# Three banks for the block sums, two for the direct sums, and POOL copying the codes of its rows

## The chip, the cores and the metric

The kernel runs on one core of a Trainium2 chip. The metric is the device time of one execution in microseconds (us), as the median of ten runs. Five engines run side by side, each through its own list of instructions in order: PE (TensorE, matrix products), DVE (VectorE), ACT (ScalarE), POOL (GpSimd) and SP (SyncE, which here only issues transfers). Transfers run on 16 DMA engines that all queues share.

## The reference

A graph layer with 6,250 nodes of 128 features and 206,250 edges. Each edge has a row of 128 numbers, which is added to the row of its source node; the node rows then go through a small network and a layer norm:

```
edge_aggr = jnp.zeros((n, HIDDEN), dtype=x.dtype).at[row].add(edge_features)
combined = jnp.concatenate([x, edge_aggr, global_expand], axis=-1) @ W_c + b_c
h = jax.nn.softplus(combined @ W1 + b1)
h = jax.nn.softplus(h @ W2 + b2)
return h @ W3 + b3
...
x = _layernorm(x + _L0_gnn_ref(x, edge_index, edge_attr_128, ...), axis=-1)
```

Nearly all the time goes into the first line, the sum of 206,250 rows by source node.

## The kernel before

**The sum by node.** The 6,250 nodes are cut into 25 blocks of `BL` = 256 nodes. The sum of each block stands transposed in SBUF, as 256 columns of `sums_t` (128 features on the partitions). An edge row is added to its block with a product on PE: the weights are 128 edge rows (edges on the partitions, features along), the moving side is a 0/1 matrix `hot` of 128 edges by 256 nodes with a one where the edge's node is. That needs 128 edges of one block together, and the edges come in no order. So the edges go through DRAM:

- The edges lie as 1,612 columns of 128. The first 48 columns (`DIRECT`) are treated apart. The other 1,564 are cut into ten groups g0 to g9 of 40, 120, 200, 240, 240, 240, 212, 140, 88 and 44 columns (`GROUPS`).
- `positions(g)` counts on PE and DVE where each edge of a group goes, so that the edges of one block lie together. It ends in a table `pos`. Its count matrices use two PSUM tiles called `pr` (two banks) and two called `small`.
- A group is loaded in pieces of ten columns (`LOAD_COLS`), 159 in all: `load_rows` (issued by SP, `LEAD` = 3 pieces ahead, five buffers) brings 10 x 128 edge rows of 128 numbers into `rows`. `code_rows` copies one number for each edge, the code `low` that says which node of the block it is, into the 129th column of `rows` (line 599, on ACT, two pieces ahead). `scatter_rows` issues, on POOL, one indirect transfer for each column (line 607): 128 rows of 129 numbers go to the places that `pos` names in a DRAM buffer `place`. There are three such buffers, filled ahead with -1 (`fill_rows`).
- `reduce_steps(g)` reads a scattered group back by loads of 1,024 rows (`load`, two ahead, four buffers `chunks`). `match` compares on DVE the 129th number of every row with 256 node numbers and gives `hot` (line 406, two buffers). `total` multiplies on PE (line 421), two block sums to a PSUM tile `part` (two buffers), and adds each to `sums_t` on DVE (line 426). `sub`, the chunk in columns, is 1, 2 or 4 by group: a load holds 8, 4 or 2 sums.

**The direct columns.** `direct_steps` makes for the first 48 columns a `direct_hot` of 128 x 512 on ACT (lines 540 and 542, three buffers), for all 13 windows of nodes, multiplies on PE (line 552) into one PSUM bank `direct_sum`, and adds that on DVE (line 556).

**The node rows.** `node_rows` prepares during one group (g3) what the network needs of `x` (28 steps with 13 loads of `x`, transposes and products in `small` tiles).

**The order of the work.** PE, DVE, ACT and SP run in the order in which the program writes the instructions down. The loop at line 659 goes through the groups, and in each through its pieces: after `load_rows(i + 3)`, `code_rows(i + 2)` and `scatter_rows(i)` of a piece it writes a share of four lists of steps: `prep` (the positions of g+1), `sums` (`reduce_steps(g - 1)`), `other` (the node rows) and `filled` (the filling). `AHEAD` says at which share of the group's pieces each list is to be through. A share of the direct steps, by the weights `left`, comes with them. Behind the loop the sums of g9 follow (line 689), and then the network and the layer norm (lines 693 to 823).

Of the kernel before, what the change touches and what calls it, by code (L numbers as in the profile page):

```python
# [7 lines left out]
F32 = mybir.dt.float32  # L8
# [28 lines left out]
AHEAD = (0.75, 0.95, 0.9, 0.75)  # L37
# [8 lines left out]
def kernel(  # L46
# [119 lines left out]
    with ExitStack() as phase:  # L166
# [4 lines left out]
        chunks_p = phase.enter_context(tc.tile_pool(name="chunks", bufs=4))  # L171
        direct_p = phase.enter_context(tc.tile_pool(name="direct", bufs=1))
        hots = phase.enter_context(tc.tile_pool(name="hots", bufs=2))
# [7 lines left out]
        low = keep.tile([P, TC], F32, name="low")  # L181
# [54 lines left out]
        def positions(g):  # L236
# [86 lines left out]
            def place(k, j0, j1):  # L323
                m = j1 - j0
                pr = by_col(ps.tile([P, 512], F32, name="pr", bufs=2))[:, :, :m]
                nc.tensor.matmul(pr, upto_h, in_block[k][1][:, :, j0:j1], start=True, stop=False)  # L326
                nc.tensor.matmul(pr, ones_h, so_far[k][:, :, j0:j1], start=False, stop=False)  # L327
                nc.tensor.matmul(
                    pr, ones_h, got["more", k].unsqueeze(2).to_broadcast([P, NB, m]),
                    start=False, stop=False)  # L330
                nc.tensor.matmul(pr, scale_h,  # L331
                                 got["begin"].unsqueeze(2).to_broadcast([2, NB, m]),
                                 start=False, stop=True)
                got[k, j0] = pr
# [49 lines left out]
        def reduce_steps(g):  # L384
# [26 lines left out]
            def total(i):  # L411
                s0, k = loads[i]
                _, at = nc.values_load_multi_w_load_instructions(
                    offs_of[g][:, s0:s0 + k], engines=[DVE], min_val=0, max_val=(NB - 1) * BL,
                    skip_runtime_bounds_check_because="it is held under the last block")
                t, hot = chunks.pop(i), hot_of.pop(i)
                for q in range(0, k, 2):
                    part = ps.tile([P, 2, BL], F32, name="part", bufs=2)
                    for s in range(q, min(k, q + 2)):
                        for j in range(sub):  # L420
                            nc.tensor.matmul(part[:, s - q, :], t[:, s * sub + j, :D],  # L421
                                             hot[:, s * sub + j],
                                             start=(j == 0), stop=(j == sub - 1))
                    for s in range(q, min(k, q + 2)):
                        here = sums_t[:, bass.ds(at[s], BL)]
                        nc.vector.tensor_add(here, here, part[:, s - q, :])  # L426
# [3 lines left out]
            for i in range(min(2, n)):  # L430
                steps.append(lambda i=i: load(i))
            for i in range(n + 1):
                def one(i=i):
                    if i + 2 < n:
                        load(i + 2)
                    if i < n:
                        match(i)
                    if i:
                        total(i - 1)
                steps.append(one)  # L440
            return steps
# [66 lines left out]
        def direct_steps():  # L508
# [26 lines left out]
            def compare(c, w, q):  # L535
                n = min(WIDE, NB * BL - w * WIDE)
                hot = direct_p.tile([P, QUAD, WIDE], F32, name="direct_hot", bufs=3)
                hot_of[c, w, q] = hot
                for j in range(QUAD):
                    nc.scalar.activation(hot[:, j, :n], iota_f[:, :n], AF.Abs,  # L540
                                         bias=less[:, w, c + q + j:c + q + j + 1], scale=-1.0)
                nc.scalar.activation(hot[:, :, :n], hot[:, :, :n], AF.Relu, bias=ones[:, :1],  # L542
                                     scale=-1.0)

            def add(c, w, q):
# [3 lines left out]
                if q == 0:  # L549
                    sum_of[c, w] = ps.tile([P, WIDE], F32, name="direct_sum", bufs=1)  # L550
# [44 lines left out]
        def code_rows(i):  # L595
            if i >= len(pieces):
                return
            g, c, k, r = pieces[i]
            nc.scalar.copy(rows_at[i][:r, :k, D:W], low[:r, c:c + k].unsqueeze(2))  # L599
# [15 lines left out]
        with tc.manual_schedule(engines={ET.PE, ET.DVE, ET.Activation, ET.SP}):  # L615
# [23 lines left out]
            for i in range(LEAD - 1):  # L639
                code_rows(i)  # L640
# [13 lines left out]
            for g in range(1, G - 3):  # L654
                left[g] = max(0.0, groups[g][1] - groups[g][0]
                              - groups[g - 1][3] * groups[g - 1][2] / 3 - (26 if g == 3 else 0))
            direct_at = 0.0
            i = 0
            for g in range(G):
# [5 lines left out]
                other = node_rows() if g == min(3, G - 1) else []  # L665
                filled = fill_rows(g + 1)
                done = [0, 0, 0, 0]
                for q in mine:
                    load_rows(i + LEAD)
                    code_rows(i + LEAD - 1)  # L670
# [4 lines left out]
                    for w, todo in enumerate((prep, sums, other, filled)):  # L675
                        share = min(1.0, (q - mine[0] + 1) / (AHEAD[w] * len(mine)))
                        upto = int(round(len(todo) * share))
                        now.append(todo[done[w]:upto])
                        done[w] = upto
# [168 lines left out]
```

## Time and profile before

| what | value |
|---|---|
| median of ten runs | 2167.57 us (2164.63 to 2169.86) |
| the profiled execution | 2164.48 us |
| its span in the trace | 2162.7 us |
| granted TensorE clock, mean | 0.915 |
| PE busy | 1768.3 us (82%) |
| PE weight loads busy | 1185.8 us (55%) |
| POOL busy | 1555.0 us (72%) |
| DVE busy | 1382.0 us (64%) |
| ACT busy | 814.6 us (38%) |
| first scatter of line 607 begins | 26.54 us |
| last scatter ends | 2007.56 us |

The profile lists, for each line of the kernel and each engine, the number of instructions, their busy time, the mean of one, and the idle time of the engine just before them with what ended it ("issue" is a wait that the profile has no releaser for). A timeline gives the same instructions in order. Busy time of POOL is what the profiler counts for an instruction; the time from one start to the next can be longer.

### The profile page before, as it was taken

The numbers are of one execution on the slowest core, as the hardware profiler recorded it, in microseconds if no ns is written. First come the engines' busy times: TensorE is split into PE (matmuls) and PEld (weight loads), VectorE is DVE, ScalarE is ACT, GpSimd is POOL, SyncE is SP. The second block draws the span as 40 slices with busy tenths as digits, with TensorE's granted clock in tenths as the row PEclk, the third lists the DMA queues.
The fourth block names the chain that finished last, engine by engine and source line by source line (L and its number), as shares of the span: only waits on it lengthen the run. The fifth ranks groups of instructions, "written<-read, shape, count | busy, mean of one in ns | idle before, by whom it ended". The sixth has DMA issues, their size and how long they took to land.

```text
span 2162.7 us, 22153 instructions
## 1 busy us (share of the span) xinstructions
PE 1768.3 (82%) x6415; PEld 1185.8 (55%) x6415; DVE 1382.0 (64%) x1943; ACT 814.6 (38%) x1174; POOL 1555.0 (72%) x1631
## 2 busy tenths in 40 slices
PE   3399798857999959999769998499993898688885
PEld 0144355534656636666446666276762777567643
DVE  7386376424767537776347764277662788798877
ACT  0367675652434444545443454434431000000034
POOL 5677777777777777777777777777777777777126
PEclk8699899978999979999979999799996999899997
DMA  9999788738888657566456555465654787787421
GB/s 290 301 302 289 204 260 255 241 100 250 252 232 254 177 151 216 190 201 215 130 181 200 191 180 174 136 211 191 198 193 141 218 232 225 197 217 203 119 81 60
DMA packets 415375, 435.49 MB, mean 201 GB/s; under 512 B 37743, under 2 KB 305766, under 8 KB 415254
## 3 DMA queue, kind: packets, MB, share of 16 engines
q1 hardware_dynamic: 365062, 330.71, 53.3%
q0 software_dynamic: 50048, 103.35, 14.4%
q8 instruction: 51, 0.84, 0.2%
q14 instruction: 70, 0.57, 0.1%
q10 hardware_dynamic: 144, 0.02, 0.0%
HBM read 260.90 MB, written 173.03 MB: 201 GB/s over the span
## 4 chain that ended last, share of the span: by engine, by line
PE 41%; DMA 19%; POOL 14%; DVE 11%; issue 10%; ACT 2%; SPq 2%; DVEq 0%; POOLq 0%; ACTq 0%
PE part L421 25%; POOL place L607 14%; PE direct_sum L552 13%; DMA place<-rows,pos 10%; DVE sums_t L426 4%; DMA chunks<-place 3%; DVE hot L406 3%; DMA x_sb<-in_x 2%; SPq L143 2%; DMA place<-fill 2%; DVE so_far L309 1%; DMA rows<-in_edge_attr 1%; PE pr L331 1%; ACT direct_hot L540 1%; ACT away L727 0%
## 5 line engine op out<-in xcount | busy, mean ns | idle before, releaser
L607 POOL DMA_INDIRECT place<-rows,pos x1564 | 1498.2, 958 | 502.2 <-issue 440.7
L421 PE MATMUL part<-hot,chunks 128*128 128x256 f32 x4472 | 1064.3, 393 | 199.5 <-DVE hot L406 167.5
L421 PEld LDWEIGHTS part<-hot,chunks 128*128 128x128 f32 x4472 | 864.5, 196 | 421.6 <-DVE hot L406 184.5
L406 DVE SCALAR_TENSOR_TENSOR hot<-chunks,iota_ps 128x2048 f32<-128x2048 f32 (+1 forms) x281 | 637.3, 2269 | 253.4 <-DMA chunks<-place 253.4
L540 ACT ACTIVATE direct_hot<-iota_f,less 128x512 f32<-128x512 f32 (+1 forms) x624 | 405.1, 696 | 679.2 <-PE direct_sum L552 676.4
L552 PE MATMUL direct_sum<-direct_hot,direct_rows 128*128 128x512 f32 (+1 forms) x1248 | 582.0, 599 | 65.1 <-DMA direct_rows<-in_edge_attr 26.6
L426 DVE TENSOR_TENSOR sums_t<-sums_t,part 128x256 f32 x781 | 327.8, 420 | 341.6 <-PE part L421 320.4
L552 PEld LDWEIGHTS direct_sum<-direct_hot,direct_rows 128*128 128x128 f32 x1248 | 239.1, 196 | 282.7 <-issue 227.2
L542 ACT ACTIVATE direct_hot<-direct_hot,ones 128x1024 f32<-128x1024 f32 (+1 forms) x312 | 348.1, 1116 | 10.1
L599 ACT COPY rows<-low 128x10 f32<-128x10 f32 (+1 forms) x159 | 31.1, 198 | 510.9 <-DMA place<-rows,pos 451.6
L342 DVE TENSOR_REDUCE pos<-at 128x20 int32<-128x500 f32 (+2 forms) x80 | 87.2, 1090 | 2.7
L309 DVE TENSOR_TENSOR_SCAN so_far<-iota_ps,ib 128x1500 bf16<-128x1500 f32 (+5 forms) x29 | 85.7, 2955 | 0.0
L556 DVE TENSOR_TENSOR sums_t<-sums_t,direct_sum 128x512 f32<-128x512 f32 (+1 forms) x52 | 34.6, 666 | 66.0 <-PE direct_sum L552 65.1
L796 POOL TENSOR_TENSOR x_sb<-x_sb,b_all 128x512 f32<-128x512 f32 (+1 forms) x13 | 15.2, 1204 | 79.1 <-DMA x_sb<-in_x 79.1
L340 DVE TENSOR_TENSOR at<-pr,ib 128x500 f32<-128x500 f32 (+2 forms) x80 | 52.8, 660 | 2.8 <-PE pr L331 2.2
L721 ACT ACTIVATE away<-z_ps 128x512 f32<-128x512 f32 (+1 forms) x13 | 7.2, 554 | 119.1 <-PE z_ps L711 119.1
L784 POOL TENSOR_SCALAR y<-y,mv,rs 128x128 f32<-128x128 f32 (+1 forms) x45 | 35.1, 792 | 18.3 <-DVE rs L778 17.5
L266 PE MATMUL small<-ib,ones_h 128*128 128x500 bf16 (+2 forms) x80 | 24.8, 421 | 24.0 <-DVE ib L255 24.0
L255 DVE TENSOR_TENSOR ib<-block,iota_ps 128x1500 bf16<-128x1500 bf16 (+5 forms) x29 | 44.2, 1548 | 0.0
L327 PE MATMUL pr<-so_far,ones_h 128*128 128x500 bf16 (+2 forms) x80 | 31.7, 396 | 13.3 <-DVE last L312 13.3
L326 PE MATMUL pr<-ib,upto_h 128*128 128x500 bf16 (+2 forms) x80 | 31.7, 396 | 9.3 <-DVE at L340 9.3
L282 DVE TENSOR_REDUCE size_f<-small 128x25 f32<-128x500 f32 x10 | 6.8, 676 | 39.4 <-PE small L266 39.4
(113 smaller groups left out, 439.6 us busy)
## 6 DMA issues: line engine op xcount, KB each, us to landing
chunks<-place SPq DMA_DIRECT2D x278, 516.0 KB, 5.9
rows<-in_edge_attr SPq DMA_DIRECT2D x155, 640.0 KB, 5.3
place<-fill SPq DMA_DIRECT2D x252, 258.0 KB, 8.5
place<-rows,pos POOLq DMA_INDIRECT x1564, 4.9
x_sb<-in_x SPq DMA_DIRECT2D x24, 256.0 KB, 5.5
direct_rows<-in_edge_attr SPq DMA_DIRECT2D x4, 768.0 KB
out<-y SPq DMA_DIRECT2D x12, 256.0 KB, 2.2
chunks<-place SPq DMA_DIRECT2D x3, 258.0 KB
```

Of the source, the lines that this page charges most:

```text
L143: ins = engine.dma_start(out, in_).ins
L255: nc.vector.tensor_tensor(ib, block[:, a:b].unsqueeze(1).to_broadcast([P, NB, n]), iota_ps[:, :NB].unsqueeze(2).to_broadcast([P, NB, n]), ...
L309: nc.vector.tensor_tensor_scan(t, iota_ps[:, 1:2].to_broadcast([P, NB * n]), in_block[k][0], 0.0, op0=ALU.mult, op1=ALU.add)
L340: nc.vector.tensor_mul(at, got.pop((k, j0)), in_block[k][1][:, :, j0:j1])
L342: nc.vector.tensor_reduce(pos[:, a - c0 + j0:a - c0 + j1], at.rearrange("p b g -> p g b"), axis=mybir.AxisListType.X, op=ALU.add)
L406: nc.vector.scalar_tensor_tensor(hot[:, :m], chunks[i][:, :m, D:W].to_broadcast([P, m, BL]), float(1 + BL * g), iota_ps.unsqueeze(1).to_br ...
L421: nc.tensor.matmul(part[:, s - q, :], t[:, s * sub + j, :D], hot[:, s * sub + j], start=(j == 0), stop=(j == sub - 1))
L426: nc.vector.tensor_add(here, here, part[:, s - q, :])
L540: nc.scalar.activation(hot[:, j, :n], iota_f[:, :n], AF.Abs, bias=less[:, w, c + q + j:c + q + j + 1], scale=-1.0)
L542: nc.scalar.activation(hot[:, :, :n], hot[:, :, :n], AF.Relu, bias=ones[:, :1], scale=-1.0)
L552: nc.tensor.matmul(sum_of[c, w][:, :n], rows_in[c][:, q + j, :], hot[:, j, :n], start=(q + j == 0), stop=(q + j == k - 1))
L607: s = nc.gpsimd.indirect_dma_start(out=dst, out_offset=bass.IndirectOffsetOnAxis(ap=at, axis=0), in_=rows[:r, j, :], in_offset=None)
```

## The change

- `code_rows` moves from ACT to POOL and from two pieces ahead to the piece itself: POOL copies the codes of piece `i` into its rows, and then issues the ten scatters of that piece. The two copies ahead of the loop go.
- `low` no longer has memory of its own: it is written over `src_i`.
- `total` is split into `product` (PE) and `add` (DVE). `part` has three buffers (`SUMS`), `hot` three, `chunks` five, and chunk loads run three ahead. The products of a load are written right behind its own `match`; the additions come when more than two sums are pending.
- `pr` goes: the positions use the two `small` tiles. With the bank that this leaves over, and one more, `part` has three banks and `direct_sum` two. `direct_hot` has four buffers.
- The node rows are spread over g3, g4 and g5, each time between 0.8 and 0.95 of the group's pieces, behind that group's `prep`; the weights `left` of the direct steps follow.

```diff
-AHEAD = (0.75, 0.95, 0.9, 0.75)
+AHEAD = (0.75, 0.95, None, 0.75)
+SUMS = 3
...
-        chunks_p = phase.enter_context(tc.tile_pool(name="chunks", bufs=4))
+        chunks_p = phase.enter_context(tc.tile_pool(name="chunks", bufs=5))
...
-        hots = phase.enter_context(tc.tile_pool(name="hots", bufs=2))
+        hots = phase.enter_context(tc.tile_pool(name="hots", bufs=3))
...
-        low = keep.tile([P, TC], F32, name="low")
+        low = src_i.bitcast(F32)
...
-                pr = by_col(ps.tile([P, 512], F32, name="pr", bufs=2))[:, :, :m]
+                pr = by_col(ps.tile([P, 4, P], F32, name="small", bufs=2)
+                            .rearrange("p a b -> p (a b)"))[:, :, :m]
...
-            def total(i):
+            def product(i, q):
+                k = loads[i][1]
+                t, hot = chunks[i], hot_of[i]
+                part = ps.tile([P, 2, BL], F32, name="part", bufs=SUMS)
+                for s in range(q, min(k, q + 2)):
+                    for j in range(sub):
+                        nc.tensor.matmul(part[:, s - q, :], t[:, s * sub + j, :D],
+                                         hot[:, s * sub + j],
+                                         start=(j == 0), stop=(j == sub - 1))
+                if q + 2 >= k:
+                    del chunks[i], hot_of[i]
+                pending.append((i, q, part))
+
+            def add():
+                i, q, part = pending.pop(0)
...
             for i in range(n):
                 def one(i=i):
+                    if i + 3 < n:
+                        load(i + 3)
+                    match(i)
+                    for q in range(0, loads[i][1], 2):
+                        product(i, q)
+
+                        while len(pending) > SUMS - 1:
+                            add()
                 steps.append(one)
...
-                hot = direct_p.tile([P, QUAD, WIDE], F32, name="direct_hot", bufs=3)
+                hot = direct_p.tile([P, QUAD, WIDE], F32, name="direct_hot", bufs=4)
...
-                    sum_of[c, w] = ps.tile([P, WIDE], F32, name="direct_sum", bufs=1)
+                    sum_of[c, w] = ps.tile([P, WIDE], F32, name="direct_sum", bufs=2)
...
-            nc.scalar.copy(rows_at[i][:r, :k, D:W], low[:r, c:c + k].unsqueeze(2))
+            nc.gpsimd.tensor_copy(rows_at[i][:r, :k, D:W], low[:r, c:c + k].unsqueeze(2))
...
-                              - groups[g - 1][3] * groups[g - 1][2] / 3 - (26 if g == 3 else 0))
+                              - groups[g - 1][3] * groups[g - 1][2] / 3 - (9 if 3 <= g < 6 else 0))
...
-                other = node_rows() if g == min(3, G - 1) else []
+                if g == 3:
+                    nodes = node_rows()
+                other = nodes[:-(-len(nodes) // (6 - g))] if 3 <= g < 6 else []
+                if 3 <= g < 6:
+                    nodes = nodes[len(other):]
...
-                    code_rows(i + LEAD - 1)
+                    code_rows(i)
                     scatter_rows(i)
...
+                        if w == 2:
+                            share = (share - 0.8) / 0.15
+                        else:
+                            share = share / AHEAD[w]
```

More of the change, by code (lines that the diff above doesn't have):

```diff
@@ L409, in match @@
                     op0=ALU.subtract, op1=ALU.is_equal)
-            def total(i):
-                s0, k = loads[i]
[L413 to L426, printed above, removed]
+            at_of = {}
@@ new lines, in reduce_steps @@
+            pending = []
+            def product(i, q):
[10 more added lines that the diff above has]
+                pending.append((i, q, part))
@@ new lines, in add @@
+            def add():
+                i, q, part = pending.pop(0)
+                s0, k = loads[i]
+                if q == 0:
+                    _, at_of[i] = nc.values_load_multi_w_load_instructions(
+                        offs_of[g][:, s0:s0 + k], engines=[DVE], min_val=0,
+                        max_val=(NB - 1) * BL,
+                        skip_runtime_bounds_check_because="it is held under the last block")
+                for s in range(q, min(k, q + 2)):
+                    here = sums_t[:, bass.ds(at_of[i][s], BL)]
+                    nc.vector.tensor_add(here, here, part[:, s - q, :])
+                if q + 2 >= k:
+                    del at_of[i]
@@ L428, in reduce_steps @@
             steps = []
             n = len(loads)
-            for i in range(min(2, n)):
+            for i in range(min(3, n)):
                 steps.append(lambda i=i: load(i))
-            for i in range(n + 1):
+            for i in range(n):
                 def one(i=i):
[L434 to L439, printed above, removed]
+                    if i + 3 < n:
[5 more added lines that the diff above has]
+                            add()
@@ L440, in reduce_steps, with end @@
                 steps.append(one)
+            def end():
+                while pending:
+                    add()
+            steps.append(end)
             return steps
@@ L595, in code_rows @@
         def code_rows(i):
-            if i >= len(pieces):
-                return
             g, c, k, r = pieces[i]
-            nc.scalar.copy(rows_at[i][:r, :k, D:W], low[:r, c:c + k].unsqueeze(2))
+            nc.gpsimd.tensor_copy(rows_at[i][:r, :k, D:W], low[:r, c:c + k].unsqueeze(2))
         def scatter_rows(i):
@@ L638 @@
             node_codes(ND, c1)
-            for i in range(LEAD - 1):
-                code_rows(i)
             for step in positions(0):
@@ L655 @@
                 left[g] = max(0.0, groups[g][1] - groups[g][0]
-                              - groups[g - 1][3] * groups[g - 1][2] / 3 - (26 if g == 3 else 0))
+                              - groups[g - 1][3] * groups[g - 1][2] / 3 - (9 if 3 <= g < 6 else 0))
             direct_at = 0.0
             i = 0
+            assert G > 6
+            nodes = []
             for g in range(G):
@@ L675 @@
                     for w, todo in enumerate((prep, sums, other, filled)):
-                        share = min(1.0, (q - mine[0] + 1) / (AHEAD[w] * len(mine)))
+                        share = (q - mine[0] + 1) / len(mine)
+                        if w == 2:
+                            share = (share - 0.8) / 0.15
+                        else:
+                            share = share / AHEAD[w]
+                        share = max(0.0, min(1.0, share))
                         upto = int(round(len(todo) * share))
```

## The prediction

> **What bounds the kernel now.** I began with the groups by line, then the busy slices, then POOL's own waits. PE is the busiest engine by its share (82%), but the line that matters is POOL's.
>
> ```profile
> POOL 5677777777777777777777777777777777777126
> ...
> L607 POOL DMA_INDIRECT place<-rows,pos x1564 | 1498.2, 958 | 502.2 <-issue 440.7
> L421 PE MATMUL part<-hot,chunks 128*128 128x256 f32 x4472 | 1064.3, 393 | 199.5 <-DVE hot L406 167.5
> ...
> L599 ACT COPY rows<-low 128x10 f32<-128x10 f32 (+1 forms) x159 | 31.1, 198 | 510.9 <-DMA place<-rows,pos 451.6
> ```
>
> The POOL row of the slices stands at the same 7 tenths from the second slice to the last but three, whatever the other engines do in them. A 7 that never moves is no sign of an engine with time to spare: 1,564 scatters with 958 ns busy and some 300 ns of "issue" each. The timeline of POOL shows it one by one:
>
> ```profile
> 908.20 0.95 POOL L607 DMA_INDIRECT place<-rows,pos  x1 [0.30 <-issue]
> 909.46 0.96 POOL L607 DMA_INDIRECT place<-rows,pos  x1 [0.30 <-issue]
> 910.72 0.96 POOL L607 DMA_INDIRECT place<-rows,pos  x1 [0.30 <-issue]
> 911.98 0.96 POOL L607 DMA_INDIRECT place<-rows,pos  x1 [0.30 <-issue]
> 913.25 0.96 POOL L607 DMA_INDIRECT place<-rows,pos  x1 [0.30 <-DVE sums_t L426]
> ```
>
> Starts are 1.263 us apart, also where another releaser than "issue" is named. The list of POOL's waits has one hole after the start:
>
> ```profile
> POOL place L607 <- issue: 440.7, 1445, 0.3
> ...
> POOL place L607 <- DMA w_sb<-in_L_gnn_W: 19.4, 1, 19.4
> POOL place L607 <- DMA place<-rows,pos: 18.9, 62, 0.3
> ...
> POOL place L607 <- DMA rows<-in_edge_attr: 6.5, 1, 6.5
> ```
>
> The columns are the total, the times and the longest wait: apart from the start and from 6.5 us at 83.5 us (the first scatter of g1, whose rows come late behind the filling) nothing is above 0.31. From the first start (26.54) to the last (2006.66) there are 1,563 steps in 1980.1 us; without the 6.2 of the hole, 1.263 each. So from 83 to 2007 us POOL sets the pace: a faster PE or DVE only waits longer for the next group. The chain of waits, which names PE for 41% of the span, follows engines that run at POOL's pace, one group behind it.
>
> Then the end. The timeline around the last groups:
>
> ```profile
> 1955.60 2.95 SPq L143 DMA_DIRECT2D chunks<-place  x4
> ...
> 1959.82 4.49 DVE L406 SCALAR_TENSOR_TENSOR hot<-chunks,iota_ps 128x2048 f32<-128x2048 f32 x2 [0.75 <-DMA chunks<-place]
> ...
> 1996.15 2.28 DVE L406 SCALAR_TENSOR_TENSOR hot<-chunks,iota_ps 128x2048 f32<-128x2048 f32 x1
> ...
> 1998.35 1.85 DVE L426 TENSOR_TENSOR sums_t<-sums_t,part 128x256 f32 x4
> ...
> 2000.11 2.28 DVE L406 SCALAR_TENSOR_TENSOR hot<-chunks,iota_ps 128x2048 f32<-128x2048 f32 x1
> ```
>
> The sums of g8 start at 1959.8, when the first read-back lands behind g8's last scatter; the last 44 scatters (g9) take 44 x 1.263 = 55.6 us of the 2007.6, so that scatter ends at 1952.0. From there DVE is without a gap, a load every 3.96 us (2.28 + 1.85, overlapping a little), until the sums of g9 end at 2085.5; 77 us of network follow. The last scatter itself ends unnoticed. The end is set by **g8's last scatter plus 211 us of DVE and the network.**
>
> **The change part by part.**
>
> *The copy on POOL.* ACT loses 159 copies (31.1 us busy, 510.9 us waited). ACT is not on the path: it waits 676.4 us for PE's direct sums besides. Gain at the end: 0. POOL gains 159 copies in its only list; 153 of them belong to g0 to g8 (4+12+20+24+24+24+22+14+9), of which g0's four lie in waits that POOL has anyway: the first in the 19.4 us, the others before the hole of 6.5. 149 count; g9's six run beside DVE's 80 us. Each copy is 128 x 10, and the first scatter behind it must wait until it is complete, since it sends what the copy writes. The trace has no copy on POOL. The nearest rows: an index fill of 128 x 13 takes 0.141 us. The addition in the network takes 0.452 us for 128 numbers on a partition and 1.267 for 512, so 2.1 ns a number above a base of 0.18, and 0.20 us for ten (it reads two inputs, the copy one). Bounds for what a piece takes longer: below, nothing, if 0.20 us fit into the 0.30 us gap that stands between two scatters in any case. If the gap stays and the copy comes on top, 0.20 with a few hundredths for the handover (0.03 to 0.04 between dependent instructions of ACT and of DVE), 0.24. If the scatter behind it needs a gap of 0.30 of its own, 0.50. Above, 0.75: the first scatter of all, which came to an idle POOL, took 1.20 us where the others take 0.96, so 0.24 more. I take **0.40**, between the two middle cases, since the wait between copy and scatter drains a queue which before was always full. 149 x 0.40 = **+59.6 us**; the ends are 0 and +112.
>
> The Trainium skill speaks on how to read such spans: "Perfetto Trace Analysis", section "GPSIMD Engine Instruction", advises to time POOL by the spacing of starts and not by the reported span. The trace agrees for the scatters (958 ns reported, 1,263 spaced), and the 0.958 us by themselves would have left 600 us of seeming slack for the copies, with a sum of about 0 for this part.
>
> A second page speaks against the change more strongly: "SBUF — State Buffer", section "Who interferes with whom", says that a DVE instruction with two inputs in SBUF fully blocks a GpSimd instruction that reads SBUF. Were line 406 such an instruction, a copy would meet it in 637 us of 1,980 and wait half of its 2.27 us: 149 x 0.32 x 1.13 = 54 us more. But its second input is `iota_ps`, a PSUM tile, and the same holds for lines 255, 309, 340 and 426; so by the page nothing is added, and no run here shows the blocking.
>
> *What the copy waits for.* It needs the piece's `rows` buffer free and `low` written; the rows were asked for three pieces (38 us) before and land in 5.3, and `low` is written a group ahead. Nothing is queued behind it but the scatters that need the same. Cost 0; if rows came late, the scatters of before would have waited too.
>
> *Products next to their match, three `part` banks, deeper loads.* The same 4,472 products, 281 matches, 781 additions and 281 loads. SP issues a load one step sooner; SP waits 1,051 us for scatters and 427 for PE as it is, never over 12 at once, and three pieces of lead (38 us) cover that. Until 1952 the gain only lengthens waits for POOL: 0. In the end part DVE loses, by the timeline, 6.6 us in waits of 0.24 to 1.11 for PE between 2029 and 2086, and 2.4 at the start of g8's sums (0.60 + 1.83). Deeper sums take away those inside, not the drain of the last. I take **-3**, between -7 and +2 (a first product that every addition of a new load still waits for).
>
> *Two `direct_sum` banks, four `direct_hot`; node rows over three groups; `pr` in `small`.* PE waited 17.7 us for DVE to free the direct bank and 12.7 for `x`, beside POOL. In g4 and g5, which take on node rows, PE is busy 266.7 and 260.7 us of 303, DVE 182.7 and 176.1; a third of 28 short steps fits. The cover is POOL's pace: 36 us of PE in each of these groups. Sharing two `small` banks could hold up the positions, but these are due at 0.75 of a group, and the node rows start at 0.8: 76 us of room for g4. Cost 0.
>
> Sum: 2164.5 + 59.6 - 3 = 2221.1 against the profiled execution. The median lies 3.1 above that execution, so **2224 us**.
>
> **The rivals.**
>
> *The copy hides in the gap (faster).* The place is the 0.30 us behind each tenth scatter, the price the 0.20 us of the copy. For it: the semaphore waits at piece ends leave no mark on the spacing now. Against: "issue" means that the profile doesn't know what the gap is, and a gap that is POOL's own work hides nothing. Then only the end part gains: 2164.5 - 3 + 3.1 = 2165, with -7, 2161. It decides below 0.02 us a piece (149 x 0.02 = 3), and faster beyond measurement needs the whole -7 or the next.
>
> *PE is the bound after all (faster).* PE waits 199.5 us ahead of line 421; if 30 us of them were on the path, the gain would be up to that: 2138 us. For it: the chain of waits with its PE 41%. Against: some 1,520 starts in a row without a hole.
>
> *The heavy handover (slower).* 0.75 a piece: 2164.5 + 112 + 3.1 - 3 = 2277. For it: the 1.20 us of the first scatter. Against: it was the first, with all else starting.
>
> *The positions come late (slower).* If the shared `small` tiles put `pos` behind the group's end, POOL gets a hole at each of nine boundaries; a `place` round costs 3 us (four products, 0.67 and 1.10 on DVE), so some 27 us, with the copies 2251. For it: two banks less for the same work. Against: the 76 us of room.
>
> **How the numbers follow.** Forecast, 0.2 to 0.6 a piece (2194 to 2254): 0.62. Heavy handover: 0.14. Late positions: 0.06. Less than 0.2 but not hidden (2169 to 2194): 0.06. Hidden: 0.09. PE the bound: 0.03. A measurement here can tell about 0.2% (4.3 us). Of the two faster cases I give 0.08 to faster and 0.04 to the same; 0.01 of the light case is the same: faster 0.08, same 0.05, slower 0.87. The range, from 0.10 a piece with -3 to 0.72 with 0: 2180 to 2275.
>
> **What would show it.** In the timeline of POOL: a copy behind every tenth scatter, and the spacing across it, 1.66 us by my price in place of 1.263; the last scatter at some 2070 us; ACT without its 451.6 us wait for scatters; PE and DVE with more idle time, not less. In the end part: under 6.6 us of DVE waits between the last sums and the network. I am wrong if the spacing across the copy stays at 1.263, or if POOL shows a hole of more than 1 us behind 84 us, or if a lower time comes with the last scatter still at 2007.

## The result and the profile after

The changed kernel takes **2181.23 us** (median of 8 runs, 2175.51 to 2183.38), the kernel before beside it 2167.52 us (28 runs): 1.0058 times as long, with a 95% interval of 1.0049 to 1.0068. That is 13.7 us more. The profiled executions are 2164.48 and 2178.05 us, their spans 2162.7 and 2176.3: 13.6 us more, so the two traces hold the whole difference. In this and all later comparisons a ratio leaves out slow runs (over 1.5% above the fastest of the same kernel), while a median is that of all runs, so a ratio can differ from the quotient of two medians.

The page of the changed kernel, with the POOL row of the 40 slices and the groups that answer to those shown of before (busy time, mean ns of one, idle time before them and its releaser):

```profile
POOL 5777777777777777777777777777777777777126
...
L629 POOL DMA_INDIRECT place<-rows,pos x1564 | 1501.6, 960 | 477.5 <-issue 414.1
L424 PE MATMUL part<-hot,chunks 128*128 128x256 f32 x4472 | 1113.9, 407 | 270.7 <-DVE hot L410 268.5
...
L410 DVE SCALAR_TENSOR_TENSOR hot<-chunks,iota_ps 128x2048 f32<-128x2048 f32 (+1 forms) x281 | 636.7, 2267 | 46.1 <-DMA chunks<-place 46.1
...
L580 DVE TENSOR_TENSOR sums_t<-sums_t,direct_sum 128x512 f32<-128x512 f32 (+1 forms) x52 | 34.7, 667 | 406.2 <-PE direct_sum L576 406.2
```

POOL keeps its 7 tenths, the scatter its 0.96 us. PE's idle time ahead of the products of the sums is 71 us longer than before (199.5 there), and the time did not grow by anything like that: these waits lie beside POOL's list. (PE's idle time in all, span less busy time, is 15 us shorter: 379.5 against 394.4.) ACT's 451.6 us of waits for scatters are gone with its copies. The new group, from the list of POOL's groups by line, and the list of POOL's waits (total, times, longest):

```profile
L621 POOL COPY rows<-src_i 128x10 f32<-128x10 f32 (+1 forms) x159 | 31.5, 211 | 2.4 <-DVE src_i L219 2.2
```

```profile
POOL place L629 <- issue: 414.1, 1358, 0.3
...
POOL place L629 <- POOL rows L621: 18.7, 120, 0.2
```

What a copy costs stands in POOL's timeline (start, duration, instruction, and in brackets the idle time ahead of it):

```profile
906.31 0.96 POOL L629 DMA_INDIRECT place<-rows,pos  x1 [0.30 <-issue]
907.57 0.96 POOL L629 DMA_INDIRECT place<-rows,pos  x1 [0.30 <-issue]
908.53 0.22 POOL L621 COPY rows<-src_i 128x10 f32<-128x10 f32 x1
908.90 0.98 POOL L629 DMA_INDIRECT place<-rows,pos  x1 [0.16 <-POOL rows L621]
910.18 0.96 POOL L629 DMA_INDIRECT place<-rows,pos  x1 [0.30 <-issue]
```

From 907.57 to 908.90 are 1.33 us where two scatters without a copy stand 1.26 apart, and the scatter behind the copy takes 0.02 more (1.28). The copy begins at the moment the scatter ahead ends, without the gap of 0.30; it takes 0.22, and the gap behind it is 0.16, not 0.30. So some 0.15 us of the copy lie where the gap was, and **0.09 us** are added. The 130 places with copies, counted over the whole trace:

| copies between two scatters | places | spacing across (median) | above 1.263 |
|---|---|---|---|
| 1 | 111 | 1.327 us | 0.064 |
| 2 | 15 | 1.446 us | 0.183 |
| 3 | 2 | 1.568 us | 0.305 |
| 4 | 2 | 1.681 us (the one that is not ahead of g1) | 0.418 |

There is a second thing in the order of these lines. Most copies do not stand directly ahead of the scatters of their own piece. POOL is not among the engines whose order the program writes by hand; the scheduling of its list put four copies, then 40 scatters, four copies again, later mostly one copy for ten scatters. Counted in the trace, 131 of the 159 copies stand one piece early, 17 two or three pieces, and 11 in their place, each of these as the first of several copies in a row. The 111 single copies are all one piece early: no scatter behind one of them sends what it wrote.

**Where the 13.6 us arise.** Each row is a moment read from the two timelines:

| moment | before | after | difference |
|---|---|---|---|
| first scatter begins | 26.54 | 25.84 | -0.7 |
| first scatter of g1 begins | 83.52 | 82.14 | -1.4 |
| last scatter of g8 ends | 1952.1 | 1964.0 | +11.9 |
| sums of g8 begin on DVE | 1959.82 | 1970.25 | +10.4 |
| sums of g9 end | 2085.50 | 2097.38 | +11.9 |
| span | 2162.7 | 2176.3 | +13.6 |

From g1's first scatter to g8's last POOL loses 13.3 us: 146 copies of 0.09. Added up place by place over this stretch, the steps across copies are 10.5 us longer than at 1.263 each, and those right behind them 2.6: 13.1 of the 13.3. The last sums neither gain nor lose against g8's last scatter. The network behind them takes 1.7 us more. There the first large products of PE took 1.87 and 1.91 us (1.04 and 1.02 before) while the granted clock was 0.64 from 2097 to 2101 us; in the same first 4 us of the network before it was 1.00. The code there is the same; why the clock was lower in these 4 us was not tested, and a single execution can't tell whether it belongs to the change.

### The profile page after: what moved, and what is told of

Read it like the earlier page. It is cut to its first block, busy times and chain, and to the rows that moved or that the text cites. A ratio compares the mean times of both kernels' runs of the same rounds, so it can differ in the third digit from the quotient of the medians.

```text
span 2176.3 us, 21410 instructions
## 1 busy us (share of the span) xinstructions
PE 1796.8 (83%) x6415; PEld 1213.4 (56%) x6415; DVE 1370.0 (63%) x1943; ACT 791.7 (36%) x1015; POOL 1589.6 (73%) x1790
## 4 chain that ended last, share of the span: by engine, by line
PE 58%; DVE 18%; DMA 7%; POOL 6%; issue 6%; ACT 1%; SPq 1%; DVEq 1%; POOLq 0%
PE part L424 39%; PE direct_sum L576 16%; DVE hot L410 8%; POOL place L629 6%; DMA place<-fill 4%; DVE sums_t L441 3%; DMA place<-rows,pos 2%; DVE so_far L312 1%; DVE sums_t L580 1%; SPq L145 1%; DMA rows<-in_edge_attr 1%; PE small L335 1%; DVE pos L346 1%; DVE ib L258 1%; DVE at L344 1%
## 5 line engine op out<-in xcount | busy, mean ns | idle before, releaser
L424 PE MATMUL part<-hot,chunks 128*128 128x256 f32 x4472 | 1113.9, 407 | 270.7 <-DVE hot L410 268.5
L424 PEld LDWEIGHTS part<-hot,chunks 128*128 128x128 f32 x4472 | 899.4, 204 | 513.7 <-DVE hot L410 333.9
L576 PE MATMUL direct_sum<-direct_hot,direct_rows 128*128 128x512 f32 (+1 forms) x1248 | 558.9, 580 | 30.6 <-DMA direct_rows<-in_edge_attr 27.2
L576 PEld LDWEIGHTS direct_sum<-direct_hot,direct_rows 128*128 128x128 f32 x1248 | 233.3, 190 | 233.3 <-issue 206.6
L344 DVE TENSOR_TENSOR at<-small,ib 128x500 f32<-128x500 f32 (+2 forms) x80 | 52.8, 661 | 4.2 <-PE small L335 3.5
L523 DVE TENSOR_SCALAR z_x<-small,z_bias 128x512 f32<-128x512 f32 (+1 forms) x13 | 9.3, 717 | 51.3 <-PE small L521 51.3
L331 PE MATMUL small<-so_far,ones_h 128*128 128x500 bf16 (+2 forms) x80 | 31.4, 393 | 11.6 <-DVE last L315 11.6
L515 DVE COPY x_t<-small 128x512 f32<-128x512 f32 (+1 forms) x13 | 8.6, 658 | 41.0 <-PE small L513 41.0
```

Source lines behind the costliest of these rows:

```text
L344: nc.vector.tensor_mul(at, got.pop((k, j0)), in_block[k][1][:, :, j0:j1])
L424: nc.tensor.matmul(part[:, s - q, :], t[:, s * sub + j, :D], hot[:, s * sub + j], start=(j == 0), stop=(j == sub - 1))
L576: nc.tensor.matmul(sum_of[c, w][:, :n], rows_in[c][:, q + j, :], hot[:, j, :n], start=(q + j == 0), stop=(q + j == k - 1))
```

## The experiments

On five of the six chips that these runs came to, the kernel before itself took 2,808 to 2,872 us; on the sixth, where the scatters were measured alone, it took 2172.26, and that one is called the quiet chip here. Ratios compare kernels on the same chip.

**The whole kernel, one part undone or altered.** Four edits. The copy back on ACT, two pieces ahead:

```diff
         def code_rows(i):
+            if i >= len(pieces):
+                return
-            nc.gpsimd.tensor_copy(rows_at[i][:r, :k, D:W], ...
+            nc.scalar.copy(rows_at[i][:r, :k, D:W], ...
...
+            for i in range(LEAD - 1):
+                code_rows(i)
...
-                    code_rows(i)
+                    code_rows(i + LEAD - 1)
```

The reverse of this in the kernel before (the copy on POOL, nothing else changed). The copy tied to its place, behind the last scatter of the piece before, by an order without a semaphore:

```diff
+            ins = nc.gpsimd.tensor_copy(rows_at[i][:r, :k, D:W], ...).ins
+            if put.get("scatter") is not None:
+                tc.add_manual_dep(ins, put["scatter"].name, NO_SYNC, ...)
...
+                put["scatter"] = s.ins
```

And every copy issued twice (`for _ in range(2):` around it). What was expected, in this order:

> The changed kernel with one part undone: the codes are copied by ACT again, two pieces ahead; all else stays as changed. Theory A (the whole loss is POOL's 159 copies, some 0.09 us each, because POOL is the pace): about 2167 us, ratio 1.000 (0.997 to 1.003), last scatter at about 2007 us. Rival B (the loss comes from the products, the banks and the node rows): ratio 1.005 or more. Rival C (the sums with three banks are worth something that the copies hide): below 0.997.

> The kernel before with one part of the change alone: POOL copies the codes, in the order that the changed kernel has. Theory A: about 2180 us, ratio 1.006 (1.004 to 1.008), last scatter at about 2019 us. Rival B: ratio below 1.002.

> The changed kernel with every copy held behind the last scatter of the piece before, so that it stands directly in front of its own ten scatters and the first of them must wait until it is complete (in the changed kernel the copies run one to three pieces ahead). Theory A1 (a copy is cheap because it fits into the 0.30 us gap, wherever it stands): within 0.2% of the changed kernel, 2177 to 2186 us, spacing across a copy 1.33 us. Theory A2 (it is cheap because it runs ahead, so that no scatter waits for its completion; the handover priced in the prediction is real): 0.40 us a piece and not 0.09, so 149 x 0.31 = 46 us more than the changed kernel, about 2227 us; anything from 2195 us up speaks for A2.

> The changed kernel with every copy issued twice (the second writes the same values). In its trace two copies in a row take 0.33 us where one takes 0.21, so theory A expects 0.12 us for each added copy, 153 x 0.12 = 18 us more than the changed kernel: about 2199 us, ratio to before 1.015 (1.012 to 1.018). If POOL is not the pace (rival B), no more than the changed kernel: ratio 1.006.

The first three were run again on a second chip, and the copy on ACT on a third:

> The changed kernel with ACT copying the codes again, two pieces ahead, once more, since in the first four runs the kernel before itself took 2814 us and POOL waited for late rows. Where the kernel before takes some 2167 us: theory A (the whole loss is POOL's copies) about 2167 us, ratio 0.997 to 1.003, last scatter at about 2007 us; rival B (products, banks, node rows cost it) 1.005 or more; rival C (the copies hide a gain) below 0.997.

> The kernel before with the copies on POOL alone, once more. Theory A: about 2180 us, ratio 1.004 to 1.008, last scatter at about 2019 us. Rival B: ratio below 1.002.

> The changed kernel with every copy held behind the last scatter of the piece before, so that the first scatter of its own piece waits for it, once more. The first run of it showed 1.46 us across a copy where 1.26 is the spacing of scatters and 1.33 to 1.35 stands in the changed kernel. So theory A2 in a smaller size (a copy that runs ahead costs 0.09 us a piece, one that is waited for 0.22): 149 x 0.13 = 19 us above the changed kernel, about 2200 us, ratio 1.015 (1.012 to 1.018). Theory A1 (no difference where it stands): ratio 1.006. The prediction's own price of 0.40: ratio 1.027.

> The changed kernel with ACT copying the codes again, two pieces ahead, a third time, since in both earlier sessions the kernel before itself took some 2,820 to 2,870 us and POOL waited for late rows. Where the kernel before takes some 2167 us: theory A (the whole loss is POOL's copies) ratio 0.997 to 1.003, last scatter at about 2007 us; rival B (products, banks, node rows cost it) 1.005 or more; rival C (the copies hide a gain) below 0.997.

The changed kernel itself and the copy on ACT went to a fourth:

> The changed kernel itself, unchanged, beside the kernel before on the chip of the experiments. Where the kernel before takes some 2167 us: 1.0058 again (1.004 to 1.008). Where it takes some 2820 us (as in the three sessions so far, with PE, DVE and ACT waiting for their own instructions in stretches of 10 to 40 us): theory A (POOL's copies cost the same there) expects the difference to the variant with the copies on ACT (1.016 to 1.022) to be small, some 0.5%; if a wait for late rows on POOL's list grows with the copies, about 1.045, as the kernel before with the copies on POOL had.

> The changed kernel with ACT copying the codes, beside the changed kernel itself. Where the kernel before takes some 2167 us: theory A (the whole loss is POOL's copies) ratio 0.997 to 1.003, last scatter at about 2007 us; rival B 1.005 or more; rival C below 0.997. Where it takes some 2820 us: 1.016 to 1.022, as before.

| kernel | chip | median, us | before there, us | ratio [95%] |
|---|---|---|---|---|
| copy on ACT | first | 2864.05 | 2813.79 | 1.016 [1.010, 1.022] |
| before, copy on POOL | first | 2932.91 | 2813.79 | 1.045 [1.040, 1.050] |
| copy tied to its piece | first | 2968.39 | 2813.79 | 1.055 [1.050, 1.061] |
| every copy twice | first | 2949.98 | 2813.79 | 1.053 [1.047, 1.058] |
| copy on ACT | second | 2909.75 | 2872.36 | 1.022 [1.004, 1.039] |
| before, copy on POOL | second | 2967.05 | 2872.36 | 1.037 [0.994, 1.080] |
| copy tied to its piece | second | 2990.28 | 2872.36 | 1.050 [1.030, 1.070] |
| copy on ACT | third | 2865.0 | 2823.06 | 1.016 [1.011, 1.022] |
| changed kernel | fourth | 2964.78 | 2807.6 | 1.057 [1.049, 1.064] |
| copy on ACT | fourth | 2871.41 | 2807.6 | 1.023 [1.016, 1.031] |

These runs missed what they were made for. The sizes expected of them are those of a kernel that POOL paces, and on these chips it doesn't. What stops there is seen in two views of the copy on ACT on the third chip: a stretch of the timeline ("remote" is what the profile names where it has no releaser of the core itself), and the busy time of each engine in two windows (us, then PE, PEld, DVE, ACT, POOL, the granted clock, the DMA share and GB/s).

```profile
1116.38 0.96 POOL L631 DMA_INDIRECT place<-rows,pos  x1 [0.31 <-issue]
1119.73 0.36 SPq L145 DMA_DIRECT2D chunks<-place  x1
...
1123.27 1.33 ACT L564 ACTIVATE direct_hot<-iota_f,less 128x512 f32<-128x512 f32 x2 [36.87 <-remote]
...
1123.49 0.69 DVE L580 TENSOR_TENSOR sums_t<-sums_t,direct_sum 128x512 f32<-128x512 f32 x1 [37.19 <-remote]
...
1126.15 0.96 POOL L631 DMA_INDIRECT place<-rows,pos  x1 [8.82 <-ACT rows L623]
```

```profile
1095.00:1105.00 10.00, 3.19 (x4) 0.87 (x5) 0.00 (x0) 0.00 (x0) 7.58 (x8) 0.59 0.16 53
1105.00:1115.00 10.00, 1.15 (x2) 0.10 (x1) 0.00 (x0) 0.00 (x0) 7.65 (x8) 0.50 0.16 53
```

DVE and ACT stand still for 37 us, PE is busy for 3.19 and 1.15 us of the two windows, SP issues nothing before 1119.73, and the DMA engines move 53 GB/s, which is what the scatters alone come to (128 rows of 516 bytes in 1.263 us are 52). POOL goes on at its 1.263, and then waits 8.82 us for ACT's copy. So on such a chip POOL has long holes; in the changed kernel's run on the fourth chip the largest entry of its waits is

```profile
POOL place L629 <- DMA rows<-in_edge_attr: 638.5, 60, 27.6
```

and with the copy on ACT, on the same chip, a scatter waits for ACT instead:

```profile
POOL place L631 <- ACT rows L623: 525.8, 74, 20.5
```

The traces tell whom the engines wait for. In each of the 14 traces from these five chips DVE and ACT have 59 to 74 waits above 10 us that the profile calls "remote" (the longest of a trace 38 to 62 us), and every one ends with an update of a semaphore that only PE's instructions update: it is PE that is held up. In the stretch above, PE's last matmuls start 1.1 to 2.8 us apart, most of the time between them being "issue", and the update that ends the waits comes 15 us after the last of them. The traces of the first measurement have no such wait, and no pause of PE above 1 us that is put to "issue". The granted clock is lower on such a chip (0.82 in this run, 0.94 in the changed kernel's trace), but PE's busy time grew only from 1,797 to 1,948 us, so the clock alone is not the 700 us.

What the table does say: on these chips the copies on POOL cost far more than 13 us (by the ratios 93 us between the two kernels on the fourth; some 126 in the kernel before, on the first), and the rest of the change costs 45 to 66 us there, by the ratios of all five runs of the copy on ACT (the fifth follows below). What holds PE up, and why a copy costs more there, the runs did not settle. The tied copies (1.45 across at the least, as on the quiet chip) were not better than those that run ahead (1.050 and 1.055 against 1.057, on different chips), so the order of the copies does not seem to be it.

**The scatters alone.** To measure the price without that interference, the kernel was cut to what POOL paces: the block sums, their read-backs and the direct columns are left out.

```diff
-            direct = direct_steps()
+            direct = []
...
-                sums = reduce_steps(g - 1) if g else []
+                sums = []
...
-            for step in reduce_steps(G - 1):
-                step()
```

Four versions of it, on the quiet chip: the copies on ACT, on POOL as changed, tied, and twice as changed.

> Leaves out the read-back, the block sums and the direct sums (the output lacks the edge sums); positions, row loads, filling, scatters, node rows and the network stay, and ACT copies the codes. With PE, DVE and ACT nearly empty POOL must be the pace whatever the chip: 1,564 scatters of 1.263 us from about 26 us, then the network: about 2085 us. This is the base for the next three. If it takes far more than 2100 us, late rows pace POOL here too.

> The same, with the copies on POOL in the order of the changed kernel (they run one to three pieces ahead). Spacings in the traces say 0.07 us across a copy and 0.02 in the scatter behind it, 0.09 us: 159 x 0.09 = 14 us above the run with ACT (12 to 17). The prediction's 0.40 would give 64 us. A rival, that POOL's copies cost nothing and the loss of 13.7 us is in the sums: below 4 us.

> The same, with each copy directly in front of its own piece's scatters, so that the first of them waits for its completion. The spacing of 1.44 to 1.46 across a copy and 0.03 in the next scatter give 0.22 us: 159 x 0.22 = 35 us above the run with ACT (31 to 39). If running ahead buys nothing: 14 us. The prediction's price: 64 us.

> The same, with every copy issued twice into the same place, so that the second waits for the first (no change of values). The smallest spacing across such a pair in the earlier run was 1.94, so 0.68 + 0.03: 159 x 0.70 = 111 us above the run with ACT (95 to 125): what a wait of one POOL instruction for the completion of another costs (0.6 us a pair beyond the copy). If the second copy only adds its own 0.12: 33 us.

| scatters only | median, us (range) | above ACT | for each of 159 copies |
|---|---|---|---|
| copies on ACT | 2090.16 (2089.83 to 2095.53) | | |
| on POOL, as changed | 2108.55 (2107.85 to 2110.64) | 18.4 | 0.116 us |
| on POOL, tied to its piece | 2123.94 (2123.0 to 2128.53) | 33.8 | 0.213 us |
| on POOL, each twice | 2138.36 (2137.1 to 2139.1) | 48.2 | 0.303 us (a pair) |

With nothing else to hold them, the copies of the second version do not keep the order of the changed kernel, as was expected, but run in fours, the first of each four right ahead of its own piece: 33 places with four copies, 1.69 us across, which is 0.45 for four with the 0.02 of the scatter behind. With the 11 places of fewer copies these make 17 us, the upper end of what was expected; the medians gave 18.4, just above it. The tied version has the order that the prediction assumed, and hit what was expected of it. Its timeline:

```profile
910.07 0.96 POOL L631 DMA_INDIRECT place<-rows,pos  x1 [0.30 <-issue]
911.04 0.21 POOL L621 COPY rows<-src_i 128x10 f32<-128x10 f32 x1
911.52 0.98 POOL L631 DMA_INDIRECT place<-rows,pos  x1 [0.28 <-POOL rows L621]
912.81 0.96 POOL L631 DMA_INDIRECT place<-rows,pos  x1 [0.30 <-issue]
```

Here the scatter needs the copy just ahead, and the gap behind the copy is 0.28 instead of 0.16. But the gap ahead of the copy is still missing. One gap, one copy: 1.45 across, 0.19 more than a plain step, with the next scatter 0.21. A wait for the copy just ahead is thus worth 0.12 us, the difference of 0.21 and 0.09.

Doubling was a miss: far less than expected. Its timeline shows the eight copies of a burst as one pipelined stretch, and, where a pair stands alone, a much larger price:

```profile
904.16 0.96 POOL L630 DMA_INDIRECT place<-rows,pos  x1 [0.30 <-issue]
905.12 1.10 POOL L622 COPY rows<-src_i 128x10 f32<-128x10 f32 x8
906.49 0.98 POOL L630 DMA_INDIRECT place<-rows,pos  x1 [0.27 <-POOL rows L622]
```

```profile
189.93 0.96 POOL L630 DMA_INDIRECT place<-rows,pos  x1 [0.30 <-issue]
190.90 0.47 POOL L622 COPY rows<-src_i 128x10 f32<-128x10 f32 x2
191.90 0.98 POOL L630 DMA_INDIRECT place<-rows,pos  x1 [0.53 <-issue]
```

Eight copies take 1.10 us, 0.14 each. In the trace the first four of this burst wait for no copy, and the last four for POOL's own semaphore: the list has the four first copies, then the four second ones, so that three other copies lie between the two of a pair, and no wait shows. At the four places where a pair stands alone, the spacing across it is 1.94 to 1.97 us, 0.67 to 0.70 above a plain step, which is what was expected of every pair. So the version does not show that a copy which writes the same place again needs no wait; the order of the list hid it at most places. Why the gap behind a single pair is 0.53 is open. Doubling added 29.8 us for 159 copies, 0.19 each.

**The other terms.** On the fifth chip: the copy on ACT and the copy on POOL alone once more; the kernel before with 60 direct columns in place of 48 (`DIRECT = 60`, the sixth group 228 columns instead of 240), 12 scatters fewer; and the copy on ACT with DVE's register load moved:

```diff
             def add():
-                if q == 0:
-                    _, at_of[i] = nc.values_load_multi_w_load_instructions(...)
...
                     match(i)
+                    _, at_of[i] = nc.values_load_multi_w_load_instructions(...)
```

> The changed kernel with ACT copying the codes, beside the other three, where the kernel before takes some 2,170 us again. Theory A (the whole loss is POOL's copies; the banks, the products and the node rows are beside POOL): ratio 0.998 to 1.002, last scatter at about 2007 us. Rival B (they cost it): 1.005 or more. Rival C (they gain, hidden by the copies): below 0.997.

> The kernel before with the copies on POOL alone, beside the run with ACT. Theory A: 0.09 to 0.12 us for each of 149 copies, 13 to 18 us: ratio 1.006 to 1.008. Rival B: below 1.003.

> The kernel before with 12 columns more in the direct part and 12 fewer in g5 (60 direct columns, g5 of 228). If POOL is the pace, g8's last scatter comes 12 x 1.263 = 15.2 us earlier and the end with it: ratio 0.993 (0.991 to 0.995). PE has 312 products of 0.6 us at most more, some 140 to 190 us over g1 to g6, where it was idle for 10 to 14% (some 170 us of 1,430): if PE can't hold that, POOL gets holes at the group ends and the ratio is 1.000 or more.

> As the run with ACT copies, with the load of the eight column numbers into DVE's registers moved from in front of a load's first addition to directly behind its match. In the changed kernel's trace DVE waits 0.45 us at that place in each of g9's loads. If the register load is what it waits for: some 4 us less than the run with ACT copies (9 loads x 0.45), ratio 0.996 to 0.999; if PE's product is: the same as that run.

| kernel | median, us | ratio to before (2819.58) [95%] |
|---|---|---|
| copy on ACT | 2879.44 | 1.023 [1.017, 1.029] |
| before, copy on POOL | 2941.7 | 1.042 [1.037, 1.047] |
| before, 60 direct columns | 2859.92 | 1.012 [1.007, 1.017] |
| copy on ACT, register load behind the match | 2855.53 | 1.014 [1.007, 1.020] |

The 60 columns were to show POOL's pace in the whole kernel by a gain for 12 fewer scatters. On this chip, where POOL has holes anyway, they made it slower, which tells nothing of the quiet chip. The register load explains why the waits inside g9's sums did not shrink. In the kernel before and in the changed kernel's timeline of DVE, these sums look like this:

```profile
2057.39 1.86 DVE L426 TENSOR_TENSOR sums_t<-sums_t,part 128x256 f32 x4 [0.24 <-PE part L421]
```

```profile
2060.36 2.28 DVE L410 SCALAR_TENSOR_TENSOR hot<-chunks,iota_ps 128x2048 f32<-128x2048 f32 x1
2062.55 1.85 DVE L441 TENSOR_TENSOR sums_t<-sums_t,part 128x256 f32 x4
2064.85 1.86 DVE L441 TENSOR_TENSOR sums_t<-sums_t,part 128x256 f32 x4 [0.44 <-PE part L424]
2066.62 2.28 DVE L410 SCALAR_TENSOR_TENSOR hot<-chunks,iota_ps 128x2048 f32<-128x2048 f32 x1
...
2095.53 1.85 DVE L441 TENSOR_TENSOR sums_t<-sums_t,part 128x256 f32 x4 [0.20 <-DVE sums_t L441]
```

The wait of 0.44 between two sets of four additions, where 0.24 stood before, lies where DVE reads the load's block numbers into registers (the `values_load`, now in `add`; the trace has its record there, 0.59 us from 2063.99), and the profile puts such waits now to PE, now to DVE itself. In the run with that load moved:

```profile
2752.44 2.28 DVE L410 SCALAR_TENSOR_TENSOR hot<-chunks,iota_ps 128x2048 f32<-128x2048 f32 x1
2754.64 3.81 DVE L436 TENSOR_TENSOR sums_t<-sums_t,part 128x256 f32 x8
2758.37 2.28 DVE L410 SCALAR_TENSOR_TENSOR hot<-chunks,iota_ps 128x2048 f32<-128x2048 f32 x1
2760.57 3.81 DVE L436 TENSOR_TENSOR sums_t<-sums_t,part 128x256 f32 x8
2764.29 2.28 DVE L410 SCALAR_TENSOR_TENSOR hot<-chunks,iota_ps 128x2048 f32<-128x2048 f32 x1
```

Eight additions in a row, and 5.93 us from match to match in place of 6.26. Some other loads of that run wait 0.46 us for PE instead, so from the sixth match before the short last one to that one it is 37.1 us against 38.3 with the load in its place (37.8 in the kernel before): about 1 us of gain in the end part. The medians differ by 24 us, and the six runs of the two versions hardly overlap (2832 to 2873 and 2865 to 2906), so on that chip the edit seems to help, by far more than the 4 us expected; what the rest of it is stays open. No version was shown to beat the kernel before.

## Why the prediction was wrong, step by step

**What bounds the kernel: right, on a chip like that of the profile.** POOL's plain spacing is the same 1.26 before and after, no hole of more than 1 us lies behind 84 us, and the end follows g8's last scatter: +11.9 there, +11.9 where the sums end. DVE's idle time grew by 26 us (780.7 to 806.3) without a cost. In the kernel of the scatters alone with the copies on ACT, which leaves PE, DVE and ACT little to do, POOL's plain spacing is 1.266 and its last scatter ends at 2016.4 (2007.6 before): the pace is POOL's own.

**The price of a copy: the step that failed.** The prediction took 0.40 us a piece, "since the wait between copy and scatter drains a queue which before was always full". Both halves of that were wrong. First, there is no such wait: it assumed a copy directly ahead of its own scatters, because the program's loop writes it so, while POOL's list is ordered by another hand, most copies one piece early. In the trace that is worth the difference of 0.09 and 0.21. Second, where the wait is put in by force, it costs 0.21, not 0.40: the gap of 0.30 is paid once for copy and scatter, not once each. That is the case which the prediction had worked out at 0.24 ("the gap stays and the copy comes on top") and passed over. So the term of +59.6 was 13.3; with the assumed order it would have been 149 x 0.21 = 31.

The prediction named the moment of this: the rival that the copy hides in the gap. Most of it did: 0.15 of 0.21 us. The bound "below, nothing" and the 0.24 enclose the 0.09; to weigh the middle by a story of a drained queue, for which the trace of before had no row, was the fault. What POOL does in the part of the gap that a copy can share, the runs don't say.

**The end part, -3: it came to nothing.** The waits for PE that were to go (6.4 us between 2029 and 2086 before, where the prediction has 6.6) are 6.4 us between 2038 and 2098 after. About half of these now lie at the register load, some 0.45 for a load, which the split into `product` and `add` put between additions. At the start of g8's sums the two waits are 1.68 and 2.04 us, not 0.60 and 1.83. Before and after:

```profile
1964.91 0.88 DVE L426 TENSOR_TENSOR sums_t<-sums_t,part 128x256 f32 x2 [0.60 <-PE part L421]
1967.61 0.87 DVE L426 TENSOR_TENSOR sums_t<-sums_t,part 128x256 f32 x2 [1.83 <-PE part L421]
```

```profile
1970.25 4.48 DVE L410 SCALAR_TENSOR_TENSOR hot<-chunks,iota_ps 128x2048 f32<-128x2048 f32 x2
1976.40 0.88 DVE L441 TENSOR_TENSOR sums_t<-sums_t,part 128x256 f32 x2 [1.68 <-PE part L424]
1979.32 0.88 DVE L441 TENSOR_TENSOR sums_t<-sums_t,part 128x256 f32 x2 [2.04 <-PE part L424]
```

From the start of these sums to the end of g9's it is 127.1 us, before 125.7; 1.3 of the 1.4 are these two waits. As the sums also begin 1.5 us sooner behind g8's last scatter, the part neither gains nor loses. DVE has the same matches and additions for a load in either order; that this is why three part banks and loads three ahead change nothing here was not tested.

**Parts costed at nothing: right in the two traces, not on other chips.** No hole of POOL at a group's start (the late positions), no hole for the node rows, no wait for a buffer of `rows`; the first scatter of g1 came 1.4 us sooner. But the 45 to 66 us that the change without its copies costs on the chips where the engines stop has no place in the working, and its cause is not found.

**Blocking by DVE: next to nothing, as the prediction had it.** "SBUF — State Buffer", section "Who interferes with whom", was read as adding nothing here, since line 406's second input lies in PSUM. None of the 111 single copies was spaced over 1.4 us, though DVE was busy for 63% of the span. What the prediction overlooked are short DVE instructions with all their inputs in SBUF, such as line 318 of the changed kernel, which has two (0.19 us, 19 times). The two longest of the 111 copies (0.26 and 0.27 us, 1.37 and 1.38 across) lie beside line 318 and beside lines 315 to 318; a third copy that met line 318 took its 0.21, and line 318 took 0.23. That would fit the page, but three cases of some 0.05 us are no test of it. The advice of "Perfetto Trace Analysis", section "GPSIMD Engine Instruction", to go by the spacing of starts held: the copy's reported 0.21 us would have given 33 us for 159, the spacing gave 13 to 14.

**The rivals.** Heavy handover (2277), late positions (2251), PE as the bound (2138): none of them happened. What came was the case "less than 0.2 but not hidden" (2169 to 2194), which had a chance of 0.06. That the median still lies 1 us inside the range (2180 to 2275) is luck: its lower end was worked out from 0.10 a piece with -3, and what came is 0.09 with nothing, and 1.7 us in the network that no term had. Of the marks named in advance, the copy at 1.66 us spacing (1.33) and the last scatter at some 2070 us (2019.9) failed; ACT's missing wait held, and the longer idle time for DVE; PE's is shorter in all.

**What stays open.** The copies were not undone by themselves in the whole kernel on the quiet chip: that 13.1 of the 13.6 us are theirs rests on the two traces, place by place, and on the price from the scatters alone. That POOL sets the pace there was not tried by taking scatters away.

## What to carry to other kernels

Before costing a moved instruction, find who orders the engine it moves to: an engine outside the hand-written order may run it a piece or more earlier, and then there is no wait to pay. The same goes for an experiment: look at the order that came out before reading its price. Where a list has a steady gap between instructions, price an added short instruction by both ends (wholly in the gap, wholly on top) and take neither a drained queue nor a second gap without a row that shows one. A version that leaves out all but the engine in question measures such a price to a few hundredths of a microsecond on 159 instances, where the whole kernel's times were ruled by something else.

## What the runs showed of the hardware that was not expected

- A POOL copy of 128 x 10 between two scatters that don't need it adds 0.09 us to their spacing, one that the next scatter needs 0.21, each further one in a row 0.11 to 0.14; all are reported as some 0.2.
- On five of six chips DVE and ACT have 59 to 74 waits above 10 us in an execution, all for PE, up to 38 to 62 us long, while POOL's scatters go on at 1.263 us in the stretch shown; the same kernel before takes 2,808 to 2,872 us there and 2172 on the sixth.
- Reading eight numbers into DVE's registers between two sets of additions goes with a wait of 0.45 us, in which the profile names PE or DVE as the releaser; behind a match of 2.28 us no wait shows.
